# Pinning the hand-over from the q and k stage to the v stage: last products, first softmax steps and two weight loads

## The chip, the cores and the metric

The program runs on one core of a Trainium2 chip. A core has five engines with instruction queues of their own: TensorE (PE in the profile, with its weight loads as PEld), VectorE (DVE), ScalarE (ACT), GpSimd (POOL) and SyncE (SP, here used only to issue DMA transfers). Each queue is worked off in order[...]. The metric is the device time of one launch in microseconds (us); the kernel before takes 2287.42 us in the median of 3 runs (2287.11 to 2288.5).

## The reference, cut to what matters

The input x has 384 channels of 192 x 192 pixels. Two layers follow each other.

```python
# layer 0, on gn(x), a group norm over 32 groups
qkv = einsum('bchw,oc->bohw', gn(x), w_qkv)          # 1152 channels out
qkv = max over 2x2 pixels                             # 96 x 96 pixels
qkv = 3x3 depthwise convolution(qkv)
q, k, v = split(qkv, 3)                               # 8 heads of 48 channels, 9216 positions
attn = normalised(q) @ normalised(k).T                # 48 x 48 per head
p    = sum of 4 top-k softmaxes of attn, k = 24, 32, 36, 38
out  = gelu(p @ v), doubled to 192 x 192, then w_proj
x    = x + out
# layer 1
x    = x + einsum(shifted(sign(gn(x))), sign(weight)) + bias
```

The attention matrix is over channels. So the products q times k are sums over all positions, the softmaxes work on a small matrix once, and v can only be multiplied with it after that.

## The kernel before

The image is cut into NU = 24 units of 8 rows; a unit is a 2304 KB tile xt. The kernel has four stages.

1. Statistics of the group norm over all units.
2. **q and k** (the loop that ends at L437). For each unit u there are six channel tiles m = 0 to 5 of 128 channels, 0 to 2 for q and 3 to 5 for k. `qkv_unit` (L313) computes one tile: three blocks of 6 matmuls each (fp32, so two passes for each of three K tiles) into one of three PSUM buffers named qkv (L319 to L327), a 2x2 maximum by VectorE from each buffer into the tile pooled (L328), a bias on ScalarE (L335), the first tap of the convolution on ScalarE (L342) and the other eight on VectorE (L344), and a copy of two border rows on ScalarE (L346). The result dw is transposed in 32 x 32 blocks by VectorE (L383 and L386) into the tile blocks, and `moved` (L388) sends it by 16 DMA transfers, issued by SyncE (L396 and L401), into the tile room, where positions lie on the partitions. `products(u)` (L406) multiplies q and k of a unit from room into three PSUM tiles named gram. In the loop it is called one unit late, in the middle of the next unit; for the last unit (u = 23) it is called from `gathered` (L439), which belongs to the v stage. Its first matmul can start when k's 16 transfers have landed. The last unit's tiles have 5 rows of 96 and not 4.
3. **v** (the loop L606 to L641). Each unit has three tiles, m = 0 to 2, through the same `qkv_unit`, but the convolution accumulates in a tile named chunk (L342 and L344 again, with chunk as the output). Into this loop other work is woven: `gathered()` after the second tile of unit 0 (last products, then three copies of gram to SBUF, L444, which free gram's PSUM); from unit 1 on, one step of the generator `softmaxes` (L449) per tile, 19 steps in all; and when these are through, one block of `attention` (L586) per tile. `softmaxes` begins with a reduction of the sums of squares (ss, L455) on VectorE, then a square root on ScalarE (r_qk, L188) and more small steps. Its tiles are in the pool p3.
4. The last stage, under `tc.manual_schedule()`: the projection, the signs and layer 1. It uses wg1 and wb, which are made from two weight tensors: wl is loaded by ScalarE's DMA queue (L579, L582), reduced by VectorE into wg1 (L580), and turned into signs by ScalarE into wb (L583). In the kernel before these five lines are traced ahead of the v loop.

What sets the order: stages 1 to 3 are ordered by the scheduler of the Tile layer. It goes by the order in which instructions are traced, and puts a later instruction ahead when its own model of the machine says that it is ready and the earlier one is not. The result is a fixed order in each engine's queue. Once an instruction stands in a queue, everything behind it waits for it.

The tiles of stage 2 (blocks, dw and the others) and those of stage 3 (p3 with ss, some and ones; p4w with v's pooled tiles and wl) use the same region of SBUF on the right side, one after the other. So an instruction that writes such a tile first may have to wait for the last reader of what lay there before. The transfers that `moved` issues read blocks.

Of the kernel before, what the change touches and what calls it, by code (L numbers as in the profile page):

```python
# [10 lines left out]
F32 = mybir.dt.float32  # L11
# [4 lines left out]
AF = mybir.ActivationFunctionType  # L16
ALU = mybir.AluOpType
AX = mybir.AxisListType
PSUM = bass.MemoryType.PSUM

P = 128
C = 384
CT = C // P
# [5 lines left out]
GRP = 12  # L29
# [3 lines left out]
NU = H // UR  # L33
# [4 lines left out]
TAKEN = -3e38  # L38
# [15 lines left out]
UC = 4  # L54
# [93 lines left out]
def conv_preact_kernel(ctx: ExitStack, tc: tile.TileContext, a: dict, out: bass.AP):  # L148
    nc = tc.nc
# [203 lines left out]
    with tc.tile_pool(name="p2w", bufs=1, side="right") as wp, tc.tile_pool(  # L353
        name="p2t", bufs=2, side="right"
    ) as tp:
        gram = [pg.tile([P, 512], F32, name=f"gram{t}") for t in range(CT)]


        size = -(-(PR + 1) * WP // P) * C
        blocks = wp.tile([P, 2, size], F32, name="blocks")  # L360
        nc.gpsimd.memset(blocks, 0.0)
        pool = padded(wp, 2 * CT)
        room = big.tile([P, CT, UPX], F32, name="room", tag="big").rearrange("p t n -> p (t n)")
        qkT = room[:, : 2 * size].rearrange("p (s n) -> p s n", s=2)

        def of_unit(u):

            lo, hi = rows(u)
            n = hi - lo + 1
            nk = -(-n * WP // P)  # L370
            q, k = qkT[:, 0, : nk * C], qkT[:, 1, : nk * C]
            return (
                n,
                nk,
                q.rearrange("p (t k c) -> p t k c", t=CT, k=nk),
                k.rearrange("p (b k c) -> p b k c", k=nk, c=B),
            )

        def transposed(u, s, t, acc):
            n, nk, *_ = of_unit(u)  # L380
            to = blocks[:, s, : nk * C].rearrange("p (j t k c) -> p t k j c", j=NBP, t=CT, c=B)[:, t]
            full, more = divmod(n * WP // B, NBP)
            nc.vector.transpose(to[:, :full], acc[:, : full * P].rearrange("p (k j c) -> p k j c", j=NBP, c=B))  # L383
            if more:
                src = acc[:, full * P : n * WP].rearrange("p (j c) -> p j c", c=B)
                nc.vector.transpose(to[:, full, :more], src)  # L386

        def moved(u, s):  # L388

            n, nk, q, k = of_unit(u)  # L390
            for j in range(NBP):
                src = blocks[:, s, j * nk * CT * B : (j + 1) * nk * CT * B]
                for i in range(NBP):
                    at, to = slice(i * B, (i + 1) * B), slice(j * B, (j + 1) * B)
                    if s == 0:
                        nc.sync.dma_start(  # L396
                            q[to].rearrange("p t k (i c) -> p i (t k) c", i=NBP)[:, i],
                            src[at].rearrange("p (m c) -> p m c", c=B),
                        )
                    else:  # L400
                        nc.sync.dma_start(  # L401
                            k[to].rearrange("p (t i) k c -> p i t (k c)", i=NBP)[:, i],
                            src[at].rearrange("p (t m) -> p t m", t=CT),
                        )

        def products(u):  # L406

            n, nk, q, k = of_unit(u)
            for i in range(nk):
                L = min(P, n * WP - i * P)  # L410
                for t in range(CT):
                    nc.tensor.matmul(  # L412
                        gram[t][:, : BN[t] * B],
                        q[:L, t, i],
                        k[:L, B0[t] : B0[t] + BN[t], i],
                        start=u == 0 and i == 0,
                        stop=u == NU - 1 and i == nk - 1,
                    )

        for u in range(NU):  # L420

            for v in range(u, u + KEEP + 1):
                if v not in kept:
                    kept[v] = unit(v % NU)
            xt = kept.pop(u)
            lo, hi = rows(u)
            n = hi - lo + 1
            for m in range(2 * CT):
                acc = tp.tile([P, (PR + 1) * WP], F32, name="dw")[:, : n * WP]
                qkv_unit(pqkv, xt, u, m, pool[m], [(acc, 0, n)])  # L430
                transposed(u, *divmod(m, CT), acc)
                sq = tp.tile([P, (PR + 1) * WP], BF16, name="sq", bufs=1)
                nc.scalar.activation(sq[:, : n * WP], acc, AF.Square, accum_out=ssq[:, m, u : u + 1])  # L433
                if u and m == CT - 1:
                    products(u - 1)
                if m % CT == CT - 1:
                    moved(u, m // CT)  # L437
# [11 lines left out]
    def softmaxes(p3, psp):  # L449
# [2 lines left out]
        ones = p3.tile([P, P], F32, name="ones")  # L452
        nc.gpsimd.memset(ones, 1.0)
        ss = p3.tile([P, 2 * CT], F32, name="ss")
        nc.vector.tensor_reduce(ss, ssq, AX.X, ALU.add)  # L455
        nc.vector.tensor_scalar_max(ss, ss, 1e-24)
        rn = p3.tile([P, 2 * CT], F32, name="rn")
        inv_sqrt(p3, rn, ss, 2 * CT, "qk")
# [29 lines left out]
        for i, kk in enumerate(KS):  # L488
            cut = p3.tile([P, CT, HD], F32, name=f"cut{i}")
            while out < kk:  # L490
                n = min(8 - out % 8, kk - out)
                for t in range(CT):
                    if out % 8 == 0:
                        nc.vector.max(m8[:, t], rest[:, t])
                    if n == 8:
                        nc.vector.match_replace(cut[:, t], m8[:, t], rest[:, t], TAKEN)
                if n < 8:

                    nc.vector.memset(some, TAKEN)
                    nc.vector.tensor_copy(some[:, :, :n], m8[:, :, out % 8 : out % 8 + n])  # L500
                    for t in range(CT):
                        nc.vector.match_replace(cut[:, t], some[:, t], rest[:, t], TAKEN)
                rest, out = cut, out + n
                yield
            left.append(cut)
# [65 lines left out]
    with ExitStack() as vs:  # L571
# [2 lines left out]
        p3 = right("p3", stack=scratch)  # L574
        vs.enter_context(products_of_x)
        pool = padded(wp, CT)

        wl = wp.tile([P, CT, C], F32, name="wl")
        nc.scalar.dma_start(wl, a["w_projG"].rearrange("(t p) o -> p t o", p=P))  # L579
        nc.vector.tensor_reduce(wg1, wl.rearrange("p t (g c) -> p t g c", c=GRP), AX.X, ALU.add)  # L580
        wl = wp.tile([P, CT, C], F32, name="wl")
        nc.scalar.dma_start(wl, a["weightT"].rearrange("(t p) o -> p t o", p=P))  # L582
        nc.scalar.activation(wb, wl, AF.Sign, saturate=False)  # L583
        done, steps = 0, None

        def attention(g):  # L586

# [18 lines left out]
        for u in range(NU):  # L606
            xt = kept.pop(NU + u) if NU + u in kept else unit(u)
            if u == NU - 1:
                kept[u] = xt
                for i, f in enumerate(FIRST):  # L610
                    kept[f] = unit(f, big if i else early)
            if u % UC == 0:
                chunk.append(big.tile([P, CT, CPX], F32, name="chunk", tag="big"))
            lo, hi = rows(u)
            first = PR * u - 2 + lo
            last = first + hi - lo
            for m in range(CT):
                parts = []
                for c in range(first // CR, last // CR + 1):
                    r0, r1 = max(first, c * CR), min(last, c * CR + CR - 1)  # L620
                    parts.append(
                        (chunk[c][:, m, (r0 - c * CR) * WP : (r1 + 1 - c * CR) * WP], r0 - first, r1 + 1 - r0)
                    )
                qkv_unit(pqkv, xt, u, 2 * CT + m, pool[m], parts)
                if u == 0 and m == 1:
                    gathered()
                    po = vs.enter_context(tc.tile_pool(name="p4o", bufs=NP, space=PSUM))
                    psp = vs.enter_context(tc.tile_pool(name="p3ps", bufs=1, space=PSUM))
                    bg = psp.tile([P, P], F32, name="p3ps")[:NG, :1]
                    group_sums(bg, bpr.unsqueeze(2))  # L630
                    nc.vector.tensor_scalar_mul(bg1, bg, -1.0 / GRP)
                if u >= TOPK and steps is None:
                    steps = softmaxes(p3, psp)
                if steps:
                    if next(steps, 1):
                        steps = ()
                        scratch.close()
                        early = opened("p5x0", 1)
                elif steps == () and done < NAB - HOLD and (done + 1) * ABLK <= first * WP:
                    attention(done)  # L640
                    done += 1  # L641
# [216 lines left out]
```

## Time and profile before

| what | value |
|---|---|
| time, median of 3 | 2287.42 us |
| span of the profiled run, mean granted clock of TensorE | 2286.9 us, 0.964 |
| PE busy | 2101.7 us, 92% |
| DVE busy | 1903.2 us, 83% |
| ACT busy | 819.4 us, 36% |
| DMA, both queues of data | 36.8% of 16 engines |
| matmuls of qkv (L321) | 3888, 1684.0 us busy |

Read the busy shares as averages only. The line of 40 slices shows where an engine that is busy nearly everywhere is not; a slice is 57.2 us. Three places are of interest for PE: the first slices (statistics, PE has nothing to do), one slice in the middle, and the last slices, in which the transfers are at their busiest. For a change that moves instructions from one place in a queue to another, the questions are which engine stands still at that place, what it waits for, and what stands behind it.

### The profile page before, as it was taken

How to read it: one execution, taken by the hardware profiler on the slowest of the kernel's cores; microseconds unless marked ns; L12 is line 12 of the kernel's file. 1: busy time of each engine (PE TensorE's matmuls, PEld its weight loads, DVE VectorE, ACT ScalarE, POOL GpSimd, SP SyncE). 2: the span in 40 equal slices, each digit the busy share in tenths (PEclk: the TensorE clock that was granted, in tenths of full speed). 3: DMA queues.
4: the chain of work that ended last, by engine and by line, in shares of the span. 5: the costliest groups of instructions: out<-in, count | busy, mean ns of one | idle time of the engine just before them, and what ended most of it. 6: DMA issues, size and time to landing. Idle time of an engine off the chain costs nothing.

```text
span 2286.9 us, 19474 instructions
## 1 busy us (share of the span) xinstructions
PE 2101.7 (92%) x6135; PEld 993.8 (43%) x6135; DVE 1903.2 (83%) x3269; ACT 819.4 (36%) x1418; POOL 211.4 (9%) x338
## 2 busy tenths in 40 slices
PE   1029999999999999999999979999999999999998
PEld 0014444444444444444444434444444444455554
DVE  4657888888888888888888878986787887889998
ACT  5532222222222222222222212225323233487775
POOL 0000000000000000000000000000000000286674
PEclk7559999999999999999999989999999999999999
DMA  9962222232222232222232222104221212289996
GB/s 398 417 261 60 66 63 70 66 102 69 66 63 71 66 101 70 66 64 70 68 99 70 66 48 83 42 18 189 83 83 67 99 42 83 83 333 404 423 412 248
DMA packets 208727, 300.30 MB, mean 131 GB/s; under 512 B 162000, under 2 KB 164848, under 8 KB 208624
## 3 DMA queue, kind: packets, MB, share of 16 engines
q1 hardware_dynamic: 197936, 243.46, 30.8%
q10 hardware_dynamic: 10688, 55.61, 6.0%
q8 instruction: 48, 0.79, 0.1%
q14 instruction: 55, 0.45, 0.1%
HBM read 213.68 MB, written 56.62 MB: 118 GB/s over the span
## 4 chain that ended last, share of the span: by engine, by line
PE 78%; DVE 11%; DMA 7%; ACT 2%; issue 1%; SPq 1%; ACTq 0%; POOL 0%; POOLq 0%; DVEq 0%
PE qkv L321 65%; DMA xt<-in_x_dram 7%; PE l1ps L743 5%; DVE chunk L344 4%; PE yps L559 3%; PE gram L412 3%; DVE pooled L328 2%; PE ops L594 2%; DVE xt L568 2%; DVE dw L344 1%; DVE stats L248 1%; DMA out_dram<-xt 1%; ACT signs L723 1%; SPq L401 0%; DVE xt L751 0%
## 5 line engine op out<-in xcount | busy, mean ns | idle before, releaser
L321 PE MATMUL qkv<-xt,wq 128*128 128x512 f32 x3888 | 1684.0, 594 | 0.3 <-DVE small L294 0.3
L321 PEld LDWEIGHTS qkv<-xt,wq 128*128 128x128 f32 x3888 | 737.1, 191 | 921.6 <-issue 825.1
L344 DVE SCALAR_TENSOR_TENSOR dw<-pooled,small,dw 128x384 f32<-128x384 f32 (+2 forms) x1152 | 709.2, 616 | 118.8 <-ACT dw L342 93.7
L328 DVE TENSOR_REDUCE pooled<-qkv 128x128 f32<-128x512 f32 x648 | 442.7, 684 | 73.6 <-PE qkv L321 73.1
L344 DVE SCALAR_TENSOR_TENSOR chunk<-pooled,small,chunk 128x384 f32<-128x384 f32 (+3 forms) x696 | 370.5, 546 | 74.7 <-ACT chunk L342 57.3
L346 ACT COPY pooled<-pooled 128x196 f32<-128x196 f32 x207 | 73.7, 356 | 764.5 <-DVE dw L344 543.0
L335 ACT ACTIVATE pooled<-pooled,small 128x384 f32<-128x384 f32 x216 | 133.0, 616 | 409.6 <-DVE pooled L328 402.0
L723 ACT ACTIVATE signs<-xt,nmean 64x1536 fp8e4<-64x1536 f32 x144 | 226.5, 1573 | 61.5 <-PE yps L559 50.3
L743 PE MATMUL l1ps<-signs,wb 128*128 128x384 fp8e4 x864 | 150.6, 329 | 6.2 <-POOL signs L715 4.5
L568 DVE SCALAR_TENSOR_TENSOR xt<-yps,small,xt 128x768 f32<-128x768 f32 x132 | 127.9, 1013 | 23.8 <-PE yps L559 19.6
L559 PE MATMUL yps<-chunk,wpr 128*128 128x384 f32 x396 | 136.5, 490 | 5.5 <-DVE xt L568 5.5
L751 DVE SCALAR_TENSOR_TENSOR xt<-l1ps,small,xt 128x768 f32<-128x768 f32 x144 | 135.6, 1008 | 6.3 <-ACT signs L723 3.6
L248 DVE BATCH_NORM_STATS2 stats<-xt 128x6 f32<-128x512 f32 x144 | 87.2, 675 | 60.4 <-DMA xt<-in_x_dram 60.4
L198 PE MATMUL gsps<-sums,small 128*32 128x2 f32 x6 | 0.5, 196 | 128.5 <-DVE sums L269 128.5
L433 ACT ACTIVATE sq<-dw 128x384 bf16<-128x384 f32 (+2 forms) x144 | 75.3, 523 | 117.0 <-DVE dw L344 117.0
L743 PEld LDWEIGHTS <-wb 128*128 128x128 fp8e4 x864 | 84.1, 97 | 74.0 <-issue 16.3
L302 POOL MEMSET pooled<- 128x196 f32 x9 | 2.4, 265 | 1173.3 <-DVE dw L344 1155.8
L342 ACT ACTIVATE dw<-pooled,small 128x384 f32<-128x384 f32 (+2 forms) x144 | 100.5, 698 | 2.3
L559 PEld LDWEIGHTS yps<-chunk,wpr 128*128 128x128 f32 x396 | 72.6, 190 | 61.0 <-PE yps L559 16.4
L239 ACT ACTIVATE junk<-xt 128x1536 bf16<-128x1536 f32 x48 | 71.1, 1482 | 52.3 <-DMA xt<-in_x_dram 51.1
L383 DVE STREAM_TRANSPOSE blocks<-dw 128x384 f32<-128x384 f32 (+1 forms) x144 | 82.0, 570 | 3.4
L412 PE MATMUL gram<-room 128*128 128x160 f32 (+3 forms) x438 | 68.1, 309 | 15.4 <-DMA room<-blocks 15.4
(117 smaller groups left out, 640.1 us busy)
## 6 DMA issues: line engine op xcount, KB each, us to landing
xt<-in_x_dram SPq DMA_DIRECT2D x83, 2304.0 KB, 12.8
out_dram<-xt ACTq DMA_DIRECT2D x19, 2304.0 KB, 14.4
room<-blocks SPq DMA_DIRECT2D x736, 36.0 KB, 2.0
xt<-in_x_dram SPq DMA_DIRECT2D x18, 768.0 KB, 8.0
out_dram<-xt ACTq DMA_DIRECT2D x9, 768.0 KB, 7.9
out_dram<-xt SPq DMA_DIRECT2D x6, 768.0 KB, 6.6
wq<-in_w_qkvT_dram ACTq DMA_DIRECT2D x1, 1728.0 KB, 15.0
room<-blocks SPq DMA_DIRECT2D x32, 48.0 KB, 2.1
```

Source lines behind the costliest of these rows:

```text
L248: nc.vector.bn_stats(stats[b][:, t, at : at + 6], xt[:, t, j * 512 : (j + 1) * 512])
L321: nc.tensor.matmul(ps, wq[:, t, m * P : (m + 1) * P], x4[:, t, r0 : r0 + nr, c0 : c0 + ncol], start=(t == 0), stop=(t == CT - 1),)
L328: nc.vector.tensor_reduce(pl[:, 2 + r0 // 2 : 2 + (r0 + nr) // 2, 1 + c0 // 2 : 1 + (c0 + ncol) // 2], ps.rearrange("p (i a j b) -> p i j ...
L335: nc.scalar.activation(new, new, AF.Identity, bias=bq[:, m : m + 1])
L342: nc.scalar.activation(acc2, src, AF.Identity, bias=bdw[:, m : m + 1], scale=wdw[:, m, 0:1])
L344: nc.vector.scalar_tensor_tensor(acc2, src, wdw[:, m, k : k + 1], acc2, ALU.mult, ALU.add)
L412: nc.tensor.matmul(gram[t][:, : BN[t] * B], q[:L, t, i], k[:L, B0[t] : B0[t] + BN[t], i], start=u == 0 and i == 0, stop=u == NU - 1 and i ...
L559: nc.tensor.matmul(ps, wpr[:, t, m * P : (m + 1) * P], o[:, t, :], start=(t == 0), stop=(t == CT - 1),)
L568: nc.vector.scalar_tensor_tensor(x5[:, m, r], yb, bpr[:, m : m + 1], x5[:, m, r], ALU.add, ALU.add)
L723: nc.scalar.activation(rows_of(sg, p, SAT[t] - HSHIFT[t][h]), xt[p, t, :].rearrange("p (r w) -> p r w", w=W), AF.Sign, bias=nmean1[p, t : ...
L743: nc.tensor.matmul(ps[:, j, : 2 * W], wb[:, t, m * P : (m + 1) * P], rows_of(sg, slice(0, P), SAT[t])[:, r0 + 2 * j : r0 + 2 * j + 2], sta ...
L751: nc.vector.scalar_tensor_tensor(blk, ps[:, :, : 2 * W], bl1[:, m : m + 1], blk, ALU.add, ALU.add)
```

## The change

It pins instructions. `tc.keep_in_program_order(ins)` adds an edge from `ins` to the instruction that was traced before it on the same engine. The edge fixes the order in the queue and makes nothing wait for completion. The scheduler can then no longer put `ins` ahead of that instruction.

- `gathered()` is called after the third tile of unit 0 and not after the second, and the last unit's matmuls of `products` are pinned there.
- The first reduction of the softmaxes (ss) is pinned behind the VectorE work of unit 1's first tile; the two memsets of some (L499) are pinned behind what is traced before them.
- The loads of wl, the reduction to wg1 and the sign to wb leave the place ahead of the v loop. The first pair comes after the first tile of unit 4 (UC = 4), the second after the first tile of unit 5, all pinned.

It is for keeping instructions that have to wait for the last transfers of the q and k stage from standing in front of v's work in the queues of PE, DVE and ACT.

```diff
@@ products
-                    nc.tensor.matmul(
+                    ins = nc.tensor.matmul(
                         gram[t][:, : BN[t] * B],
...
                     )
+                    if u == NU - 1:
+                        tc.keep_in_program_order(ins)
@@ softmaxes
-        nc.vector.tensor_reduce(ss, ssq, AX.X, ALU.add)
+        tc.keep_in_program_order(nc.vector.tensor_reduce(ss, ssq, AX.X, ALU.add))
...
-                    nc.vector.memset(some, TAKEN)
+                    tc.keep_in_program_order(nc.vector.memset(some, TAKEN))
@@ ahead of the v loop
-        wl = wp.tile([P, CT, C], F32, name="wl")
-        nc.scalar.dma_start(wl, a["w_projG"].rearrange("(t p) o -> p t o", p=P))
-        nc.vector.tensor_reduce(wg1, wl.rearrange("p t (g c) -> p t g c", c=GRP), AX.X, ALU.add)
-        wl = wp.tile([P, CT, C], F32, name="wl")
-        nc.scalar.dma_start(wl, a["weightT"].rearrange("(t p) o -> p t o", p=P))
-        nc.scalar.activation(wb, wl, AF.Sign, saturate=False)
+        def weights(name):
+            wl = wp.tile([P, CT, C], F32, name="wl")
+            tc.keep_in_program_order(nc.scalar.dma_start(wl, a[name].rearrange("(t p) o -> p t o", p=P)))
+            return wl
@@ the v loop, after qkv_unit
-                if u == 0 and m == 1:
+                if m == 0 and u == UC:
+                    wl = weights("w_projG").rearrange("p t (g c) -> p t g c", c=GRP)
+                    tc.keep_in_program_order(nc.vector.tensor_reduce(wg1, wl, AX.X, ALU.add))
+                if m == 0 and u == UC + 1:
+                    tc.keep_in_program_order(nc.scalar.activation(wb, weights("weightT"), AF.Sign, saturate=False))
+                if u == 0 and m == CT - 1:
                     gathered()
```

## The prediction

> **What bounds the kernel now.** I read the page first, for the engine that is busy nearly everywhere and for where it is not.
>
> ```profile
> PE 2101.7 (92%) x6135; PEld 993.8 (43%) x6135; DVE 1903.2 (83%) x3269; ACT 819.4 (36%) x1418; POOL 211.4 (9%) x338
> PE   1029999999999999999999979999999999999998
> DVE  4657888888888888888888878986787887889998
> PEclk7559999999999999999999989999999999999999
> ```
>
> PE is the bound from the fourth slice on, with one dent, in the 24th slice (1315 to 1372 us), where the granted clock dips too. Then the windows view, cut at the borders of the stages (columns: length, then busy time and instructions of PE, PEld, DVE, ACT, POOL, then the clock, the DMA share and GB/s):
>
> ```profile
> 1299.00:1344.40 45.40, 45.40 (x118) 21.24 (x117) 42.70 (x70) 10.27 (x20) 1.35 (x12) 1.00 0.17 31
> 1344.40:1381.70 37.30, 21.86 (x68) 11.87 (x68) 19.32 (x44) 5.16 (x10) 1.21 (x2) 0.77 0.19 53
> 1381.70:1970.00 588.30, 586.60 (x1667) 252.01 (x1665) 486.33 (x1007) 190.59 (x426) 2.21 (x2) 1.00 0.21 81
> ```
>
> From 1381.7 to 1970 PE lacks 1.7 us; the hand-over before it is the only large hole between statistics and last stage. PE's timeline says what is in it:
>
> ```profile
> 1316.02 28.49 PE L321 MATMUL qkv<-xt,wq 128*128 128x512 f32 x66
> 1344.44 0.35 PE L198 MATMUL p3ps<-small 128*32 128x1 f32 x6
> 1360.24 0.87 PE L412 MATMUL gram<-room 128*128 128x160 f32 x2 [15.45 <-DMA room<-blocks]
> 1360.90 9.90 PE L321 MATMUL qkv<-xt,wq 128*128 128x512 f32 x18
> 1370.64 3.37 PE L412 MATMUL gram<-room 128*128 128x192 f32 x22
> 1373.84 15.62 PE L321 MATMUL qkv<-xt,wq 128*128 128x512 f32 x36
> ```
>
> A tile is 18 matmuls. So the 66 are the last 48 of q and k and v's first tile; the 18 are v's second; of the 36 the first 18 are v's third and the others unit 1's first. PE stands still for 15.45 us with the first gram matmul at the head of its queue, since k's 16 transfers land at 1360.1, and v's second tile is behind it. The other queues, from the waits view of 1344.4 to 1374:
>
> ```profile
> PE gram L412 <- DMA room<-blocks: 15.4, 1, 15.4
> DVE ss L455 <- DMA room<-blocks: 11.3, 1, 11.3
> ACT pooled L335 <- DMA room<-blocks: 7.5, 1, 7.5
> ACT r_qk L188 <- DVE ss L456: 6.1, 1, 6.1
> ```
>
> DVE stands with ss at its head: ss lies where blocks lay, which the transfers still read. ACT stands before v's first bias (L335), whose data DVE had ready at 1349; what is ahead of it in the queue is the issue of the first wl load (1354.29), and wl lies in that region as well. Then r_qk waits for ss, with v's first tap (L342) behind it. Moving gram alone would thus leave v's first tile stuck in ACT and DVE: all three pins are needed.
>
> **What the Trainium skill says.** Two places bear on this. "Perfetto Trace Analysis", section "Sequencer Loop": an engine's instruction is queued and waits there for its semaphores; this trace agrees, since v's 18 matmuls, which need nothing from the transfers, start right after gram's first two at 1360.90. "TensorE: Matmul & The Clock Gate", section "What's actually happening": the clock falls to half after an idle window of about 3.4 us and returns after as long a busy one, and the windows are free-running. The trace agrees on the half and on the fall, not quite on the return:
>
> ```profile
> 1344.44:1347.80 3.36, 0.35 (x7) 0.26 (x6) 3.29 (x8) 0.69 (x2) 0.00 (x0) 1.00 0.00 0
> 1347.80:1360.20 12.40, 0.00 (x0) 0.00 (x0) 1.16 (x2) 0.61 (x1) 0.00 (x0) 0.50 0.43 111
> 1360.20:1364.90 4.70, 4.66 (x7) 2.38 (x8) 3.90 (x9) 1.07 (x3) 1.21 (x2) 0.50 0.00 0
> ```
>
> Half speed held for 4.7 us after the restart, which cost about 2.35 us.
>
> **The change, part by part.**
>
> *Hand-over before*: 1344.44 (v's first tile done, three PSUM buffers full) to 1381.73 (third tile done, from 1374.01 plus 18 matmuls at 46.35/108 = 0.429 us, the rate of a steady stretch of the chain): 37.3 us.
>
> *Hand-over after.* Gram is behind v's third tile, so PE goes on with the second as soon as DVE empties a buffer. DVE is still at the last k tile: its convolution and transposes end at 1347.1, and the first maximum of v (0.60) ends at 1347.8. Nothing in the diff moves that, so PE waits 3.4 us. Second and third tile: 36 x 0.429 = 15.5 us, to 1363.3. Can DVE and ACT follow? ACT's bias and tap (0.62 + 0.63) can start at 1349 with the wl load gone, then eight taps on DVE of 0.52 plus three maxima of 0.60 make 6.0 us a tile, against 7.7 of PE; yes. Chunk is no obstacle: of the eight big buffers, six hold loaded units and one is room, so it took that of unit 23, free when PE finished k at 1339. Gram: 24 matmuls at 2.60/18 = 0.144, 3.5 us, with the data there since 1360.1, 3.2 us earlier. The small matmuls of L198, now behind: 0.3. Sum 3.4 + 15.5 + 3.5 + 0.3 = 22.7 us; saved 37.3 - 22.7 = 14.6.
>
> *The clock.* The remaining gap of 3.4 us is at the edge. A gap of 3.46 us in the last stage (2006.10 to 2009.56) was followed by a clock of 0.60 for 2.4 us and 0.85 for 5 more, a loss of 2.44 x 0.40 + 5 x 0.15 = 1.7 us. Bounds 0 and 2.35; I take 0.8.
>
> *ss and some.* No instruction more or less. Some 3 us of softmax work (L455 to the first L465) move from DVE's idle time into unit 1. ss then stands behind unit 1's first tile, when the transfers are long done, and delays nothing; who waits for it is r_qk on ACT and the rest of the softmax, not needed before PE's transposes of full at 1529.
>
> *The two loads.* Reduction 1.35 us on DVE, sign 1.16 on ACT, as now, but amid v (about 1366.8 + 3 x 23.2 + 7.7 = 1444 for the first), and each may wait for its load: 5.2 and 3.7 us to landing in this trace. Behind the reduction in DVE's queue are maxima that free PSUM, and PE waits for those. In the present trace DVE is full (20.00 of 20) from 1400 to 1420 and 1440 to 1480, yet its maxima start at most 1.9 us after PE ends a block; PE, with two more buffers, loses nothing until about 4.3. Of 1.35 plus a wait of 0 to 5.2, less 2.4 in hand, 0 to 4.1 us reach PE. Behind the sign on ACT is the bias of the next tile, which DVE waits for: 0 to 2. The scheduler places both where its model has the data landed, so most of the latency should be under other work; I take 0.4 for the two.
>
> *The rest* moves along. The last stage starts from v's end (POOL waits 605.9 us for PE's qkv before it may clear the signs), and its transfers start then too, so nothing there absorbs the gain.
>
> Sum: 14.6 - 0.8 - 0.4 = 13.4 us, **2274.0 us**.
>
> **The rivals.**
>
> 1. *DVE takes part of it back.* It is full for most of 80 us already, and now gets 3 + 1.35 us more and perhaps two waits: 4.1 + 2 reach PE, the clock costs 2.35: 14.6 - 8.4 = 6.2, 2281 us. For it: the full windows. Against: PE loses nothing in them now.
> 2. *The wait only changes place.* If the load of unit 6, which waits for v's third tile (issued at 1381.76 now), got ahead of k's transfers in SP's queue, these would start at 1363.3, take 13 us (1347.1 to 1360.1 now), and gram would end at 1380: 1.7 us before the 1381.7 of now, 2286 us. Against: the transfers are traced first and ready first.
> 3. *Slower: the softmax comes too late.* From 1480 to 1520 DVE is busy 16.6 us of 20, so it has 1.3 us a tile free. The softmax work between 1400 and 1480 is 79.8 - 80 x 0.83 = 13 us; with some 4 in 1389 to 1400 (estimated from its rows there) and 4.4 moved in, about 22: 17 tiles, 131 us. Started at 1381 it would end at 1512; the attention, 14 us earlier than now, wants it at 1515. If both load waits (9 us) fall on DVE as well, it ends seven tiles (54 us) later, and PE, its queue in order, stands before the transposes for the part that DVE cannot defer; I put it at 20 us, 2294 us. For it: the sum. Against: now the same work, started at 1360, is through at 1477, 52 us ahead of need, because DVE defers taps of v, which PE doesn't wait for.
>
> **How the numbers follow.** Forecast (savings of 11 to 17.5 us) 73%, rival 1 14%, rival 2 5%, rival 3 8%. The first two are faster by over 0.2% (4.6 us), apart from a bad end of rival 1: faster 86%, same 5%, slower 9%. Range: below, the whole 15.45 us and the 2.35 of clock are saved, 2287.4 - 17.8 = 2269.6; above, all of rival 1 and a little, 2282. That leaves out rivals 2 and 3 and the tails.
>
> **What would show it.** In PE's timeline: 24 gram matmuls in one piece at about 1363, after 54 of v, and the gap before v's second tile some 3 us, ended by DVE's maximum (L328), not by a DMA; from 1344.4 to the end of gram about 23 us. In the waits: room<-blocks gone from PE, DVE and ACT; wl loads waited for near 1440 to 1475. A PE gap of over 1 us there, or before the transposes of full, is rival 1 or 3; gram still waiting for room is rival 2. The forecast is wrong if the hand-over shrinks as said and the end doesn't follow, or if the gap of 3.4 us widens since something else of v's first tile also lies on the transfers' region.

## The result and the profile after

The changed kernel takes 2275.5 us (median of 4, 2274.3 to 2277.0) against 2288.0 of the kernel before beside it; the ratio is 0.9946, 95% interval 0.9928 to 0.9963. That is 12.5 us less, where 13.4 were forecast (2274.0). The changed kernel run again on another chip gave 2274.1 against 2288.2, ratio 0.9941 (0.9927 to 0.9954).

The windows view of the changed kernel, cut at the borders of its stages (columns as before: length, busy time of PE, PEld, DVE, ACT, POOL, clock, DMA share, GB/s):

```profile
1299.00:1343.50 44.50, 44.50 (x116) 20.84 (x114) 41.83 (x69) 10.27 (x20) 1.35 (x12) 1.00 0.17 30
1343.50:1368.90 25.40, 22.27 (x67) 11.75 (x67) 17.54 (x34) 5.13 (x10) 1.21 (x2) 0.87 0.13 32
1368.90:1956.80 587.90, 586.54 (x1667) 252.02 (x1665) 487.17 (x1018) 190.46 (x426) 2.21 (x2) 1.00 0.22 83
1956.80:2272.50 315.70, 294.77 (x1336) 164.81 (x1332) 278.93 (x300) 234.75 (x169) 200.92 (x291) 0.99 0.83 337
```

The hand-over (from the end of v's first tile to the point where its third tile and gram are both done) has gone from 37.3 us to 25.4. (The 37.3 ends with the last matmul itself; the other hand-overs here end where PE's next matmul starts. Read so, it is 37.1, and the savings given below are 0.2 us smaller.) The rest of v is 587.9 us against 588.2 (1381.73 to 1969.93), and the last stage 315.7 against 317.0 (1969.93 to the end). Nearly the whole gain lies in the one place. The profiled spans differ by 14.4 us and the medians by 12.5: the profiled execution before (2288.7 us) was 0.7 over its median, the changed one (2274.3) 1.2 under. Of the 14.4, 0.9 was there before the hand-over, with the same work up to it.

PE's timeline of the changed kernel (start, length, engine, line, instructions, and in brackets the idle time before with what ended it):

```profile
1315.12 28.49 PE L321 MATMUL qkv<-xt,wq 128*128 128x512 f32 x66
1343.54 0.35 PE L198 MATMUL p3ps<-small 128*32 128x1 f32 x6
1347.02 18.59 PE L321 MATMUL qkv<-xt,wq 128*128 128x512 f32 x36 [3.13 <-DVE pooled L328]
1365.44 3.64 PE L412 MATMUL gram<-room 128*128 128x160 f32 x24
1368.92 19.91 PE L321 MATMUL qkv<-xt,wq 128*128 128x512 f32 x46
```

The gap of 15.45 us that a DMA ended is now one of 3.13 us that DVE's maximum (L328) ends. Gram is in one piece behind 54 matmuls of v and waits for nothing. But the 36 matmuls of the second and third tile take 18.4 us, start to start of gram, and not the 15.5 of full clock. The waits view of 1340 to 1385 in the changed kernel:

```profile
ACT pooled L335 <- DVE pooled L328: 22.4, 4, 8.2
POOL ones L455 <- DMA room<-blocks: 18.5, 1, 18.5
...
PE qkv L321 <- DVE pooled L328: 3.1, 1, 3.1
```

The transfers (room<-blocks) no longer hold PE, DVE or ACT. Only POOL still stands before them, with the memset of ones, which nobody needs yet.

### The profile page after: what moved, and what is told of

It reads as the page before. It is cut to its first block, busy times and chain, and to the rows that moved or that the text cites. A ratio compares the mean times of both kernels' runs of the same rounds, so it can differ in the third digit from the quotient of the medians.

```text
span 2272.5 us, 19472 instructions
## 1 busy us (share of the span) xinstructions
PE 2100.3 (92%) x6135; PEld 993.2 (44%) x6135; DVE 1902.3 (84%) x3269; ACT 819.4 (36%) x1418; POOL 211.4 (9%) x338
## 4 chain that ended last, share of the span: by engine, by line
PE 77%; DVE 11%; DMA 7%; ACT 2%; issue 1%; SPq 0%; ACTq 0%; POOL 0%; POOLq 0%; DVEq 0%
PE qkv L321 65%; DMA xt<-in_x_dram 7%; PE l1ps L749 4%; DVE chunk L344 4%; PE yps L561 3%; PE gram L412 3%; PE ops L594 2%; DVE pooled L328 2%; DVE xt L570 2%; DVE dw L344 1%; ACT signs L729 1%; DVE stats L248 1%; DVE xt L757 1%; DMA out_dram<-xt 1%; ACT chunk L342 0%
## 5 line engine op out<-in xcount | busy, mean ns | idle before, releaser
L328 DVE TENSOR_REDUCE pooled<-qkv 128x128 f32<-128x512 f32 x648 | 442.8, 684 | 73.8 <-PE qkv L321 73.4
L198 PE MATMUL gsps<-sums,small 128*32 128x2 f32 x6 | 0.5, 196 | 127.7 <-DVE sums L269 127.7
L707 POOL COPY rest<-signs 9x384 int32<-9x384 int32 (+1 forms) x144 | 72.4, 503 | 83.1 <-ACT signs L729 77.5
```

Source lines behind the costliest of these rows:

```text
L328: nc.vector.tensor_reduce(pl[:, 2 + r0 // 2 : 2 + (r0 + nr) // 2, 1 + c0 // 2 : 1 + (c0 + ncol) // 2], ps.rearrange("p (i a j b) -> p i j ...
```

## The experiments

Two theories were to be told apart first. **Three queues**: v's work stood behind an instruction that needed the last transfers in three queues (gram on PE, ss on DVE, the first wl load on ACT), so that each pin alone frees little. **Gram alone**: PE's wait is what counts, and the other pins are trimmings.

**Only the products moved and pinned** (e1).

```diff
 kernel before, plus
+                    if u == NU - 1:
+                        tc.keep_in_program_order(ins)
...
-                if u == 0 and m == 1:
+                if u == 0 and m == CT - 1:
```

> Only the move of the last products behind v's third tile, with the pins on their matmuls; softmax steps and weight loads as before. Theory (three queues hold v back, and all three must be freed): PE goes on with v's second tile at about 1347.8, but DVE still stands before ss until 1360, so the second tile's first maximum comes near 1364 and PE waits some 6 us a second time before the third tile, with the clock down again. The hand-over (v's first tile done to gram done, or to the third tile done where gram is earlier) is 33 to 36 us against 37.3 before and 25.4 after; time 2283.5 to 2287.5. Rival (PE's wait for the products is all that counts): hand-over about 25 us, time 2275 to 2277.

Measured: 2285.4 against 2288.3 us, ratio 0.9990 (0.9984 to 0.9997). PE's timeline of this kernel shows how PE runs one tile ahead and then stops again:

```profile
1346.81 10.69 PE L321 MATMUL qkv<-xt,wq 128*128 128x512 f32 x18 [3.13 <-DVE pooled L328]
1364.29 10.50 PE L321 MATMUL qkv<-xt,wq 128*128 128x512 f32 x18 [6.79 <-DVE pooled L328]
1374.63 3.64 PE L412 MATMUL gram<-room 128*128 128x160 f32 x24
```

And its waits view shows who held DVE:

```profile
DVE ss L457 <- DMA room<-blocks: 11.0, 1, 11.0
PE qkv L321 <- DVE pooled L328: 9.9, 2, 6.8
```

The transfers still end PE's wait, only at one remove: PE waits for DVE, and DVE for the transfers. The hand-over is 34.8 us. Gram alone is refuted.

**Everything but that** (e2): the softmax pins and the moved loads, with the products called after the second tile and unpinned.

```diff
 changed kernel, minus
-                    if u == NU - 1:
-                        tc.keep_in_program_order(ins)
...
-                if u == 0 and m == CT - 1:
+                if u == 0 and m == 1:
```

> Only the softmax pins and the moved weight loads; the last products are called after the second tile, unpinned, as before. Theory: gram still stands at the head of PE's queue for 15.4 us with half the clock behind it, so nothing is gained: hand-over 36 to 37.5 us, time 2286.5 to 2288.5, although DVE and ACT do v's first tile early. Rival (the waits of DVE and ACT were what cost, PE's only the last link): time 2276 to 2281.

Measured: 2286.2 against 2288.3 us, ratio 0.9992 (0.9983 to 1.0001), no change that can be told. From PE's timeline:

```profile
1357.59 0.87 PE L412 MATMUL gram<-room 128*128 128x160 f32 x2 [14.05 <-DMA room<-blocks]
```

PE still stands before the transfers, and the hand-over is 35.7 us. It is shorter than before since the wait is 14.05 and not 15.45 us, 1.4 less: the transfers land sooner (last section). The profile thus came out slightly under the range that was written for it, the time 0.3 us under.

**Products and softmax pins, loads as before** (e5), and **products and loads, softmax unpinned** (e6).

```diff
 e5: e1, plus
+        tc.keep_in_program_order(nc.vector.tensor_reduce(ss, ssq, AX.X, ALU.add))
...
+                    tc.keep_in_program_order(nc.vector.memset(some, TAKEN))
 e6: changed kernel, minus these two pins
```

> Products moved and pinned, ss and some pinned, the weight loads ahead of the v loop as before. Theory: ACT stands before the issue of the first wl load until about 1354.3, then DVE stands behind its first tap before the reduction to wg1 until wl lands at about 1359.5; the second tile's first maximum is near 1362, PE waits about 4 us before the third tile; hand-over 30 to 33 us, time 2280 to 2283. Rival (the loads stand in nobody's way that matters): as after, 25.4 us, 2275.5.

> Products moved and pinned, loads moved, ss and some not pinned. Theory: DVE stands before ss from 1349 to 1360, then does the small softmax steps ahead of v's taps; the second tile's first maximum is near 1365, PE waits 6 to 7 us before the third tile; hand-over 33 to 36 us, time 2283.5 to 2287. Rival (the loads were the larger obstacle): 27 to 29 us, 2277 to 2279.

Measured: e5 2282.4 us, ratio 0.9974 (0.9962 to 0.9985), hand-over 32.1 us; e6 2285.6 us, ratio 0.9990 (0.9981 to 0.9999), hand-over 34.3 us. The second stop of PE is 4.64 us in e5 and 5.86 in e6. In e5 it is ACT that stands before the transfers for 7.5 us and DVE that then waits 7.1 us for v's first tap; in e6 it is DVE with ss for 9.8 us. So the parts don't add: by the hand-over, gram alone saves 2.5 us, with the softmax pins 5.2, with the loads 3.0, and with both 11.9. The last pin is worth 6.7 to 10.3 us, whichever it is, because it frees the last queue. The differences among e1, e5 and e6 hold up to 1 us that is not the pins': the half clock after PE's two stops takes 5.4, 4.9 and 5.9 us of these hand-overs (an estimate: the lengths of the two tiles, less twice the 7.89 us that 18 matmuls take in e1 at full clock).

**Products pinned behind the second tile** (e4).

```diff
 changed kernel, with
-                if u == 0 and m == CT - 1:
+                if u == 0 and m == 1:
```

> The changed kernel with the last products pinned behind v's second tile and not its third. Theory: PE is through with the second tile at about 1357 to 1358.5, the transfers land at about 1358.7 to 1360, so gram waits up to 2 us; hand-over (to the third tile's end) 26.5 to 28 us, time 2276 to 2278. Rival (the position among v's tiles is what matters most): PE waits 5 us or more with the clock down again, hand-over over 30 us, time over 2280.

Measured: 2276.8 us, ratio 0.9952 (0.9938 to 0.9965). Gram waits 1.44 us for the transfers, and the hand-over is 25.7 us, 0.3 more than behind the third tile and under what was expected. PE's timeline shows that the 0.3 flatters it:

```profile
1347.70 9.46 PE L321 MATMUL qkv<-xt,wq 128*128 128x512 f32 x18 [3.13 <-DVE pooled L328]
1358.60 3.71 PE L412 MATMUL gram<-room 128*128 128x160 f32 x24 [1.44 <-DMA room<-blocks]
```

The gap before the second tile is the same 3.13 us, but the half clock behind it cost 1.6 us here and 3.0 in the changed kernel (see the clock, in the next section). With equal losses this place would be some 1.7 us worse (an estimate, 0.3 + 3.0 - 1.6), about what gram waits. The times can't settle it, since the intervals of the two kernels overlap. What counts most is that gram isn't ahead of the second tile.

**Matmuls that fill the gap** (e3), to see whether the slow tiles come from the clock. Their results are never read.

```diff
 changed kernel, plus
+    warm = last_products.enter_context(tc.tile_pool(name="warm", bufs=1, space=PSUM)).tile([P, 512], F32, name="warm")
...
                 qkv_unit(pqkv, xt, u, 2 * CT + m, pool[m], parts)
+                if u == 0 and m == 0:
+                    for i in range(3):
+                        tc.keep_in_program_order(
+                            nc.tensor.matmul(warm, wq[:, 0, :P], xt[:, 0, :512], start=True, stop=True)
+                        )
```

> The changed kernel, with three more fp32 matmuls (unit 0's x with a slice of the qkv weights, into a PSUM bank of their own, never read) pinned behind v's first tile, so that PE has 2.6 us of work in the gap of 3.1 us. Theory (the 3.0 us that the second and third tile took over their 15.5 are the half clock after that gap): the two tiles take 15.5 and not 18.4, hand-over 22.4 us and not 25.4, time 3 us under the changed kernel, 2272 to 2273. Rival (they wait for DVE's maxima or for weights, not for the clock): the tiles still take over 17.5 us and the time stays at 2275 to 2276.

Measured: 2273.0 against 2287.8 us, ratio 0.9937 (0.9925 to 0.9950). The windows view of 1347 to 1353, first of the changed kernel:

```profile
1347.00:1350.00 3.00, 2.98 (x4) 1.45 (x5) 1.58 (x3) 1.24 (x2) 0.00 (x0) 0.50 0.26 66
1350.00:1353.00 3.00, 3.00 (x5) 1.05 (x5) 2.56 (x5) 0.36 (x1) 0.00 (x0) 0.52 0.33 82
```

and then of the kernel with the filling:

```profile
1347.00:1350.00 3.00, 2.50 (x6) 1.25 (x7) 1.61 (x4) 1.24 (x2) 0.00 (x0) 1.00 0.26 66
1350.00:1353.00 3.00, 3.00 (x8) 1.33 (x7) 2.79 (x6) 0.36 (x1) 0.00 (x0) 1.00 0.32 81
```

The granted clock (third column from the end) is 0.50 and 0.52 after the gap of 3.13 us, and 1.00 with the gap filled to 0.93 us. The two tiles then take 15.5 us, from a start 0.5 us later, and the hand-over 22.9. The 3 us of the tiles are the clock's. In the times this gain can't be told from noise: 2273.0 lies 1.1 and 2.5 us under the two medians of the changed kernel, and the intervals overlap.

**A tap of the last unit of q and k on GpSimd** (e8), to take away DVE's lateness, which makes the gap.

```diff
 changed kernel, in the taps of qkv_unit, with tp passed in from the q and k loop
+                elif u == NU - 1 and m < 2 * CT - 1 and k == 1:
+                    t2 = tp2.tile([P, (PR + 1) * WP], F32, name="tap")[:, : n * WP].rearrange("p (r w) -> p r w", w=WP)
+                    nc.scalar.mul(t2, src, wdw[:, m, 1:2])
+                    nc.gpsimd.tensor_add(acc2, acc2, t2)
```

> The changed kernel; in the last unit of q and k, for tiles 0 to 4, the second tap is made by ScalarE (a product into a tile of its own) and added by GpSimd, so that DVE has five taps of 0.73 us less. Theory (the gap that is left is DVE's lateness with k's last tile): DVE ends k's transposes some 3.5 us earlier, PE's gap after v's first tile goes below 0.5 us, the clock stays up, the transfers land by 1357 and gram follows the third tile at once: hand-over 19 to 20 us, time 2268.5 to 2270.5. Rival (GpSimd's addition is so slow, or slows DVE so much beside it, that DVE is no earlier): gap still 3 us, time 2275 or more.

Measured: 2280.2 us, 4.7 over the changed kernel, ratio to before 0.9969 (0.9958 to 0.9981). The theory's forecast failed, and not by the rival's way either. One addition takes 1.20 us on POOL, and DVE's taps are as long as ever; but the waits view of 1295 to 1350 has a new line:

```profile
DVE dw L348 <- POOL dw L346: 8.9, 5, 2.8
```

DVE stands in its own queue before taps whose first summand comes by way of ACT and then POOL. The 3.65 us of work taken off DVE came back as 8.9 us of waiting; PE's gap grew to 6.35 us and the hand-over to 27.7. So this kernel doesn't say what an earlier DVE would bring.

**Two more PSUM banks for v's second tile** (e9, and the same kernel again as e11), to leave DVE late but not have PE wait for it.

```diff
 changed kernel, with
+    more_banks = last_products.enter_context(tc.tile_pool(name="qkv2", bufs=2, space=PSUM))
...
-            ps = pqkv.tile([P, 512], F32, name="qkv")
+            ps = (first if first and c0 == 0 else pqkv).tile([P, 512], F32, name="qkv")
...
-                qkv_unit(pqkv, xt, u, 2 * CT + m, pool[m], parts)
+                qkv_unit(pqkv, xt, u, 2 * CT + m, pool[m], parts, more_banks if (u, m) == (0, 1) else None)
```

> The changed kernel; the first two blocks of v's second tile in unit 0 go to two PSUM banks of their own (the two that lie idle until the last products are done), so that PE need not wait for DVE to empty one of the three qkv buffers. Theory (the gap that is left is PE waiting for a PSUM buffer, behind a DVE that is 3.4 us late, and the clock falls in it): PE goes from the first tile into the second without a gap, the clock stays up, the two tiles take 15.5 us, gram follows at about 1360 with the transfers landed at 1358.5, hand-over 19.3 to 20 us against 25.4, time 6 us under the changed kernel, 2269 to 2270.5. Rival (DVE, not the buffers, sets the pace: its lateness comes back at the third tile, or at gram, which then waits for the transfers): hand-over 22 us or more, time 2272 or more.

> The changed kernel itself once more, so that it stands beside the others on one chip: 2274.5 to 2276.5, hand-over 25 to 25.8 us with the second and third tile at 18.4 us. If the 3 us of half clock depend on where the gap falls in the clock's windows, the two tiles may take anything from 15.5 to 19 us here, with the same gap of 3.1 us.

Measured beside each other: e9 2271.9 us (2269.5 to 2275.9), ratio 0.9930 (0.9917 to 0.9942); the changed kernel (e10) 2274.1 (2273.4 to 2276.7), its hand-over again 25.4 with the gap of 3.13 us at the same point. PE's timeline of e9:

```profile
1315.88 43.94 PE L321 MATMUL qkv<-xt,wq 128*128 128x512 f32 x102
1359.66 3.64 PE L413 MATMUL gram<-room 128*128 128x160 f32 x24
1363.22 0.35 PE L198 MATMUL p3ps<-small 128*32 128x1 f32 x6
```

102 matmuls without a gap, the last 48 of k and all three tiles of v, at full clock. The hand-over is 19.0 us, 6.4 less than in the changed kernel, as the theory said: DVE catches up within the hand-over. But the time fell only by 2.3 us in the median. In the profile v ends 5.3 us earlier (1951.5 against 1956.8), and the last stage takes 319.8 us and not 315.9: PE's wait there for DVE's second residual addition is 4.5 us and was 2.1. The same kernel was run once more.

> The kernel with two banks of their own once more. In its first profile the hand-over was 19.0 us, 6.4 less than in the changed kernel, but the last stage took 319.8 us against 315.7 to 316.6 in the other profiles, and its times spread over 6.4 us. Theory (the last stage's transfers fell badly in that one execution): the last stage takes about 316 us here, the hand-over 19 us, the span about 2267 to 2269, the time of most executions 2268.5 to 2271. Rival (an earlier start of the last stage gives the gain back there for good): last stage near 320 us again, median 2272 or more.

Measured: 2272.5 us (2270.0 to 2273.2), ratio 0.9928 (0.9915 to 0.9942); hand-over 19.0 us, last stage 319.3 us, a single wait of 3.8 us at the same place. The rival holds for the profiled executions: 3.4 to 3.9 us come back in the last stage. PE's timelines show where, first of e10, then of e9:

```profile
2013.51 3.11 PE L749 MATMUL l1ps<-signs,wb 128*128 128x384 fp8e4 x18 [2.12 <-DVE xt L757]
2010.49 5.92 PE L750 MATMUL l1ps<-signs,wb 128*128 128x384 fp8e4 x18 [4.45 <-DVE xt L758]
```

Behind the longer wait the granted clock was 0.50, so that the 18 matmuls took 5.92 us and not 3.11 (4.72 in e11). In e9 PE comes into the stage 5.3 us ahead of e10 and leaves these matmuls 0.25 us ahead. In e9 the chain of waits leads there through a load of x that took 9.42 us, in e11 through one of 9.35. The ten times of e9 and e11 lie between 2269.5 and 2275.9, four of them at 2270.2 or below, 3.2 us under the fastest of the changed kernel (2273.4). Why PE waits longer there after an earlier start, and whether the quicker of these ten executions escape it, stays open. The medians of all ten and of the nine runs of the changed kernel (2272.2 and 2274.4) are 2.3 us apart; by its medians this is the fastest version here, though its intervals overlap those of the changed kernel and of e3.

## Why the prediction was right

**The reading of the three queues** is shown. The sum assumed that all must be freed, and e2, e5 and e6 each leave one in place and e1 leaves two, and they gain 1.6 to 5.2 us of hand-over where all three gain 11.9.

**The hand-over, term by term** (forecast, then measured): the wait for DVE 3.4 and 3.5 us (with the small matmuls of L198, which stayed in front and hid in it, so their 0.3 is not there); second and third tile with the clock's loss 15.5 + 0.8 and 18.4; gram 3.5 and 3.5. Forecast 23.5, measured 25.4.

**The mis-sized term is the clock.** The prediction took 0.8 us between bounds of 0 and 2.35, out of a gap "at the edge". The gap brought the clock down in full, and PE ran at half speed from 1347.0 to 1352.9, which cost 3.0 us, over the upper bound. That bound came from the single restart in the trace of before, 4.7 us at half speed. What a restart costs is not one number, though. The windows view of the changed kernel (two lines) and of e4 (two lines), cut just inside the changes of the clock:

```profile
1343.90:1346.00 2.10, 0.00 (x0) 0.00 (x0) 2.03 (x5) 0.39 (x1) 0.00 (x0) 1.00 0.00 0
1346.10:1352.80 6.70, 5.79 (x7) 2.52 (x8) 4.85 (x11) 1.81 (x5) 0.00 (x0) 0.50 0.25 64
1347.40:1350.70 3.30, 3.00 (x4) 1.48 (x5) 1.87 (x4) 1.24 (x2) 0.00 (x0) 0.50 0.24 60
1350.80:1353.00 2.20, 2.20 (x6) 0.95 (x5) 2.09 (x5) 0.36 (x1) 0.00 (x0) 1.00 0.34 85
```

After the same gap of 3.13 us, half speed lasted 6.8 us in the changed kernel (and in e1, e6 and e10) and 3.4 us in e4 (and in e5). In the kernel before it was 17.1 us and in e2 13.7: twice, once, five and four times 3.4 us. The Trainium skill ("TensorE: Matmul & The Clock Gate", section "What's actually happening") gives windows of about 3.4 us that run freely, and these lengths agree with it. So the most likely reading is that the loss depends on where in such a window PE comes back: it was busy at half speed for 5.9 us in the changed kernel and for 3.0 in e4. On the fall the same section and the traces differ. It gives an idle window of about 3.4 us as the condition; here the clock fell 2.1 us after PE's last matmul (1343.9 to 1346.0), and in the kernel before, which the prediction read as agreeing, 3.1 us after it. The size of a loss at such an edge can't be read from one restart; e3 shows that all of it was the clock.

**The loads** were put at 0.4 us, with up to 6 in the bounds. They cost PE nothing: between the hand-over and v's end PE's waits in the changed kernel are for aT, dg and one block of the attention, 1.4 us in all. ACT waited 0.6 us for the second load, and DVE's reduction not at all. The scheduler had put other work in front of both, as forecast. In the kernel before, full is finished at 1483.5, not at 1477 as the third rival has it. In the changed kernel it is finished at 1489, still 28 us ahead of the transposes at 1516.9. So the third rival failed, with that margin.

**The first rival** (DVE takes part back, 2281 us) failed where it said: DVE is full from 1400 to 1420 and 1440 to 1460 in the changed kernel too, and PE loses nothing in either. **The second** (the wait changes place) failed as well: room<-blocks ends no wait of PE.

**The rest of the sum**: in the profiles 11.9 us from the hand-over, 0.3 in v, 1.3 in the last stage; the medians differ by 12.5. Forecast were 13.8 from the hand-over with the clock's loss, less 0.4 for the loads, and nothing elsewhere. That the total came out as near as it did is in part luck: the last stage's 1.3 us stood in no term. The clock accounts for them again, as PE's timelines show, first of before, then of the changed kernel:

```profile
2009.56 7.40 PE L743 MATMUL l1ps<-signs,wb 128*128 128x384 fp8e4 x34 [3.46 <-POOL signs L715]
1996.47 5.74 PE L749 MATMUL l1ps<-signs,wb 128*128 128x384 fp8e4 x34 [3.47 <-POOL signs L721]
```

This is the gap from which the prediction took its 1.7 us of loss. Of the same length, it cost nothing in the changed kernel, where the clock stayed at 1.00. In e1, e4, e5 and e6 the 34 matmuls took 5.74 us too, in e2, e3 and e8 again 7.40. That the last stage would absorb nothing held for this change. It did not hold for the next 6 us (e9, e11).

## What to carry to other kernels

When one late transfer feeds several consumers, look at the head of every engine's queue and at what stands behind it: work that needs nothing from the transfer may be held in three queues at once, and freeing one or two moves the stop to the next. Of a gap that remains on TensorE, count the half clock after it as well as its length, and as a range: gaps of 3.13 us cost 1.6 to 3.0 us here, gaps of 3.47 us 0 or 1.7. Filling the gap with matmuls that nobody reads, or better with real ones by lending idle PSUM banks, took that loss away. Before moving a tap or a sum to an idle engine, ask whether the busy engine then has to wait for it in its own queue.

## What the runs showed that was not expected

**A weight load delayed the transfers that everybody waited for.** In the kernel before, the chain of waits has the last of k's transfers at

```profile
1356.73 3.37 DMA room<-blocks
```

and in e2, with the wl load moved away, at

```profile
1355.49 1.96 DMA room<-blocks
```

The load of 576 KB was issued at 1354.3, among the last of the 16 transfers, and the DMA busy share in those microseconds rose to nine tenths. Without it, the last transfer takes 1.4 us less. It is the loads and not the softmax pins: the slowest of the 16 took 4.9 and 5.2 us from issue to landing in e1 and e5, where the loads stay, and 2.1 us in e6 and in the changed kernel, where they are moved. That moving the loads also shortens the transfers had no place in the prediction. In the changed kernel nobody gains by it, since gram is reached only at 1365.4.
